# A two-direction graph-attention kernel: batch 0's self feature by block products, narrow matmuls for the key rows, and another order of a batch's loads

## The chip, the cores and the metric

The kernel runs on one core of a Trainium2 chip. A core has five engines that run their own instruction streams: TensorE (PE; its weight loads are listed apart as PEld), VectorE (DVE), ScalarE (ACT), GpSimd (POOL) and SyncE (SP), which here issues nearly all DMA transfers. Each engine works through its stream in order and waits on semaphores for the others. The metric is the device time of one execution in microseconds (us); less is better.

## The reference

For each of B = 16 batches there are N = 512 tokens of F = 512 features. A linear layer makes `self_feat` from the tokens and one condition vector per batch (left out for a token whose row sums to zero). Then come two graph attentions, one on the adjacency and one on its transpose. Each has H = 16 heads of width dh = 32, and only the first NG = 20 tokens are keys:

```python
row_zero = exp_v.sum(-1) == 0
q_exp = jnp.where(row_zero[..., None], 0.0, q[:, None, :])
self_feat = jnp.concatenate([exp_v, q_exp], -1) @ W_self.T + b_self
output = self_feat
for d in range(2):
    A = adj_f if d == 0 else jnp.swapaxes(adj_f, 1, 2)
    A = A[:, :, :NONGT, :]                       # B, N, 20 keys, 11 labels
    cond, vb = A.sum(-1), A @ w_bias + b_bias
    kv = self_feat[:, :20]
    qh = (self_feat @ Wq[d].T + bq[d]).reshape(B, N, H, dh)
    kh = (kv @ Wk[d].T + bk[d]).reshape(B, 20, H, dh)
    aff = jnp.einsum('bnhd,bmhd->bnhm', qh, kh) / sqrt(dh)
    aff = jnp.where(cond[:, :, None, :] > 0, aff, NEG) + vb[:, :, None, :]
    w = softmax(aff)
    out_t = jnp.einsum('bnhm,bmf->bnhf', w, kv)
    output += jnp.einsum('bnhf,hgf->bnhg', out_t, Wout[d]) + bout[d].reshape(H, -1)
return exp_v + relu(output)
```

All is fp32. The host passes x also transposed, and the adjacency already cut to the 2 x 20 columns that are used.

## The kernel before, in words

Features lie on the 128 partitions in C = 4 chunks, tokens in the free dimension. Instead of the queries, the kernel computes for each batch and head a key matrix folded with Wq (`g`, 608 columns in each of 4 chunks: 16 heads x 2 directions x 19 keys, the first key being subtracted from the others), so that the scores are one matmul of self_feat with `g`. Likewise the values are folded with Wout (`vd`). Work is written for each engine in program order under a manual schedule: the order in the code is the order on the engine.

*The setup* (L453 to 759) loads the weights, computes the key sums (`kv_terms`, L531 to 535: 16 matmuls of 128 x 320 into four banks, 320 = 16 batches x 20 keys) and the key rows (`key_rows(d, jc)`, L577 to 592: four matmuls of 128 x 320 into a bank, then ACT and DVE make `kh0` and `khD` from it). Then come 22 *bursts* (`keys(runs)`, L660 to 695), numbered n = 0 to 21. A burst is twelve short matmuls into two double banks. ACT copies one pair out (L684), DVE the other (L686) into `st`, which goes to the scratch `g_d` by DMA. From n = 4 on, fillers stand between the bursts, by the letters of the string `plan` (L714): b biases, c bias scores, n row flags (one matmul that gives `nz`), v and w values, s one step of the direct product for batch 0's self_feat (`self_feat`, L191 to 208: the F x 472 remaining token columns in four blocks of outputs x tokens; three blocks as fillers, the fourth, `self_feat(0, 1, 1)`, in the loop). `self_copy` (L210 to 218) adds the condition part on DVE when it takes a block from its bank. In the setup, banks come from a pool of four in turn (`bank(name)`); in the loop they are fixed (`bank(name, at)`).

*The loop* (L781 to 963) runs over batches b and four token tiles nt. For tile nt: `scores` (L353, 128 narrow matmuls), then on DVE `weigh` (add the mask term `full`, maximum, difference), exp on ACT, `normal` (sum, reciprocal, and the product on POOL), `turn` (transpose, L415). POOL's `full_add` makes `full` ahead of it. `attend` (L426) and `finish` (adds on DVE, relu on ACT) for batch b - 1 stand in nt 2 of batch b, the `residual` adds (POOL) and stores behind them. In the same tiles the next batch is prepared: the mask terms (`mask_mul` on ACT, `mask_count` and `mask_sum` on DVE), `new_self` (a small ACT copy) and self_feat by seven block products (`product(b, n)`, L246 to 279, of 2 x 2 blocks, in the order n = 1, 2, 6, 7, 5, 4, 3). The operands are sums of blocks that POOL makes (`x_sum` for the tokens, `weight_sums`, once, for the weights). Products 1, 6, 7 and 4 accumulate in two banks `ps_a`, product 2 in `ps_d`, 5 and 3 in `ps_c`. Between them DVE reads `ps_a` with `partial` (two instructions, L286; it adds the condition part and writes a tile `u`), and `joined` (one instruction, L296) adds `ps_d` or `ps_c` to `u` and writes the block of self_feat.

*The loads* of batch b + 1 go through SP's one queue, in program order, some held back until an instruction is done (`behind`): two of x (nt 0), the store of the row flags, `adj` first half (behind the masks), `nz` (nt 1, behind exp), four of `cq`, `adj` second half (behind `normal`), two of `xn` for batch b + 2 (nt 2, behind the first add and the first relu of `finish`), `g` first half (behind exp), two stores, `g` second half (nt 3, behind the masks), a store, four of `vd`, a store.

Of the kernel before, what the change touches and what calls it, by code (L numbers as in the profile page):

```python
# [18 lines left out]
def gat_kernel(  # L19
# [71 lines left out]
    adds, fulls, wts, outs, held, sf_ps, conds, prods = {}, {}, {}, [], [None] * 3, {}, {}, {}  # L91
    sums, parts, us, done = {}, {}, {}, {}
# [98 lines left out]
    def self_feat(b, f, h, parts=((0, range(C)), (1, range(C)))):  # L191


        lo, hi = max(NG, h * N // 2), (h + 1) * N // 2
        for i, ks in parts:
            if (i, ks[0]) == (0, 0):
                if (f, h) == (0, 0):
                    new_self(b)
                held[0] = bank(f"ps_sf{b}_{f}{h}", 3 if (f, h) == (1, 1) else None)
            for k in ks:  # L200
                for a in range(HL):
                    nc.tensor.matmul(  # L202
                        held[0][bass.ts(a, R), i * N // 2 : i * N // 2 + hi - lo],
                        ws_v[:, k, bass.ds((2 * f + i) * P + a * R, R)], xs[b][:, k, lo:hi],
                        start=(k == 0), stop=(k == C - 1),
                    )
            if (i, ks[-1]) == (1, C - 1):
                sf_ps[b, f, h] = held[0]

    def self_copy(b, f, h):  # L210

        lo, hi = max(NG, h * N // 2), (h + 1) * N // 2
        ps = sf_ps.pop((b, f, h))
        for i in range(2):
            nc.vector.scalar_tensor_tensor(
                sfs[b][:, 2 * f + i, lo:hi], nzs[b][:, lo:hi], qw[:, 2 * f + i, b : b + 1],
                ps[:, i * N // 2 : i * N // 2 + hi - lo], ALU.mult, ALU.add,
            )

# [15 lines left out]
    def x_sum(b, n):  # L235

        t = sums[b, n] = xsum.tile([P, 2, HN], F32, tag=f"t{n}", name=f"t{b}_{n}")
        one, two = {
            1: lambda: (x_block(b, 0, 1), x_block(b, 0, 0)),
            2: lambda: (x_block(b, 1, 1), sums[b, 1]),  # L240
            3: lambda: (x_block(b, 1, 1), x_block(b, 0, 1)),
            4: lambda: (x_block(b, 1, 0), sums[b, 2]),
        }[n]()
        nc.gpsimd.tensor_sub(t, one, two)  # L244

    def product(b, n):  # L246
# [11 lines left out]
        if n == 1:  # L258
            parts[b, "a"] = [bank(f"ps_a{b}_{i}", i) for i in range(2)]
        if n == 2:  # L260
            parts[b, "d"] = bank(f"ps_d{b}", 2)
        if n == 5:
            parts[b, "c"] = bank(f"ps_c{b}", 3)
# [17 lines left out]
    def partial(b, n, f, l, to=None):  # L281

        if to is None:
            to = us[b, n] = xsum.tile([P, 2, HN], F32, tag=f"u{n}", name=f"u{b}_{n}")
# [9 lines left out]
    def joined(b, n, key, f, l):  # L294

        nc.vector.tensor_add(  # L296
            block(b, f, l), parts[b, key][:, : 2 * HN].rearrange("p (i n) -> p i n", i=2), us.pop((b, n))
# [155 lines left out]
    with tc.tile_pool(name="setup", bufs=1) as sp, tc.tile_pool(name="ps_acc", bufs=4, space=PSUM) as acc["pool"]:  # L453
# [18 lines left out]
        with tc.tile_pool(name="setup_k", bufs=1) as sk:  # L472
# [58 lines left out]
            def kv_terms(fc, k):  # L531
                nc.tensor.matmul(  # L532
                    kv_ps[fc][:, :BM], ws_v[:, k, bass.ts(fc, P)], xkv[:, k],
                    start=(k == 0), stop=(k == C - 1),
                )
# [41 lines left out]
            def key_rows(d, jc):  # L577

                ps = bank(f"ps_k{d}{jc}")
                for k in range(C):  # L580
                    nc.tensor.matmul(  # L581
                        ps[:, :BM], wk_sb[d][:, k, bass.ts(jc, P)], kvT[:, k],
                        start=(k == 0), stop=(k == C - 1),
                    )
# [26 lines left out]
        with tc.tile_pool(name="setup_g", bufs=4) as sg:  # L611
# [85 lines left out]
            def self_step(b, f, h, i, k):  # L697
                self_feat(b, f, h, ((i, (k,)),))
                if (i, k) == (1, C - 1):
                    self_copy(b, f, h)  # L700
# [6 lines left out]
                "s": [  # L707
                    (self_step, (0, f, h, i, k)) for f, h in ((0, 0), (1, 0), (0, 1))
                    for i in range(2) for k in range(C)
                ],  # L710
# [3 lines left out]
            plan = "bvv vv vv ccw vv ns ssss sssw vv vv ssss ssss vv vv nww ssss ssss".split()  # L714
# [13 lines left out]
            for n, runs in enumerate(bursts):  # L728
# [40 lines left out]
    with tc.manual_schedule():  # L769
# [11 lines left out]
        for b in range(B):  # L781
# [7 lines left out]
            for nt in range(NT):  # L789
# [22 lines left out]
                if nt == 0:  # L812
# [4 lines left out]
                    else:  # L817
# [5 lines left out]
                        partial(b, 4, 1, 0, block(b, 1, 0))  # L823
# [8 lines left out]
                        joined(b, 3, "c", 1, 1)  # L832
# [21 lines left out]
                if nt == 1:  # L854
                    if b > 0:
                        joined(b, 2, "c", 0, 1)
# [189 lines left out]
```

## Time and profile before

| | us |
|---|---|
| median of 3 runs | 591.52 (590.48 to 591.87) |
| the profiled execution's own time | 593.27 |
| its span, first to last instruction | 591.5 |
| TensorE busy | 578.7 (98% of the span) |
| VectorE busy | 492.3 (83%) |
| ScalarE busy | 395.6 (67%) |
| GpSimd busy | 384.2 (65%) |
| setup, bursts with fillers (41.1 to 92.5) | 51.4 |
| loop from batch 0's last tile on (129.4 to 560) | 430.6 |

The times come from one profiled execution. Its chain is the work that ended last, followed back at each step to what released it. A row of the chain gives start, duration, engine, tile and line; "issue" is time in which an engine waited for nothing that the profile shows. A row of the timeline gives start, duration, engine, line, operation, output <- inputs, shape, count and, in brackets, the idle time before it with what ended it. A row of windows gives the stretch, its length, then busy time (and number) of PE, PEld, DVE, ACT and POOL, the granted clock of TensorE, the DMA engines' mean share and GB/s. A DMA row gives the count, KB each and the median us from issue to landing.

### The profile page before, as it was taken

To read this page: it belongs to the slowest core of one execution; us is meant where nothing else is said; L and a number is where in the kernel's file an instruction comes from. 1 tells how busy PE (TensorE), PEld (TensorE's weight loads), DVE (VectorE), ACT (ScalarE), POOL (GpSimd) and SP (SyncE) were. 2 spreads that over 40 slices of the span, in tenths; PEclk is the share of its full clock that TensorE was granted. 3 is DMA by queue.
4 is the path that set the end of the run, shared out by engine and by line. 5 is a ranking of instruction groups with operands and counts; after the bars stand their busy time and mean duration, and the time that the engine had idled before them with its cause. 6 is when DMAs were issued, how large, how long until landed. Compare 5 with 4: busy or idle time off the path is not lost.

```text
span 591.5 us, 30038 instructions
## 1 busy us (share of the span) xinstructions
PE 578.7 (98%) x13180; PEld 439.7 (74%) x13180; DVE 492.3 (83%) x785; ACT 395.6 (67%) x1162; POOL 384.2 (65%) x351
## 2 busy tenths in 40 slices
PE   8999999999999999999999999999999999999994
PEld 6654547888978687787878787788787878787882
DVE  0495565889898888999999999888989898989896
ACT  1234644587877677768686868677787877777661
POOL 2315663638677675758686777675858677776774
PEclk9999999999999999999999999999999999999997
DMA  8998999857848485767676766757585748582503
GB/s 294 385 406 299 332 376 329 257 126 199 223 154 229 155 236 148 206 168 209 184 208 163 223 173 202 171 181 208 164 217 170 216 149 232 158 238 85 167 13 142
DMA packets 98129, 124.10 MB, mean 210 GB/s; under 512 B 19952, under 2 KB 70160, under 8 KB 95952
## 3 DMA queue, kind: packets, MB, share of 16 engines
q1 hardware_dynamic: 96752, 120.31, 67.1%
q8 instruction: 103, 1.69, 1.2%
q0 software_dynamic: 672, 1.36, 1.0%
q10 hardware_dynamic: 576, 0.53, 0.3%
q14 instruction: 26, 0.21, 0.1%
HBM read 82.30 MB, written 40.24 MB: 207 GB/s over the span
## 4 chain that ended last, share of the span: by engine, by line
PE 94%; DVE 3%; DMA 1%; issue 1%; ACT 0%; POOL 0%; SPq 0%; DVEq 0%; POOLq 0%; ACTq 0%
PE ps_s L353 44%; PE ps_a L279 17%; PE ps_c L279 8%; PE ps_o L426 6%; PE ps_d L279 4%; PE ps_v L644 3%; PE ps_k L581 3%; PE ps_sf L202 2%; DMA ws_q<-in_wsT 1%; PE ps_kv L532 1%; DVE o L435 0%; PE ps_nz L186 0%; DVE wt L415 0%; DVE ps_s L371 0%; DVE sm L406 0%
## 5 line engine op out<-in xcount | busy, mean ns | idle before, releaser
L353 PEld LDWEIGHTS ps_s<-g,sf 128*32 128x32 f32 x8192 | 264.0, 110 | 19.8 <-issue 12.2
L353 PE MATMUL ps_s<-g,sf 128*32 128x152 f32 x8192 | 277.3, 293 | 0.5 <-ACT st L684 0.5
L334 ACT COPY both<-add 32x80 f32<-32x80 f32 x512 | 130.9, 256 | 54.8 <-DVE add L325 49.0
L408 POOL TENSOR_TENSOR s<-s,sm 128x640 f32<-128x640 f32 x63 | 80.3, 1275 | 98.0 <-DVE sm L407 98.0
L341 POOL TENSOR_TENSOR full<-cq,both 128x640 f32<-128x640 f32 x64 | 100.1, 1565 | 30.3 <-issue 24.3
L314 ACT ACTIVATE prod<-adj,wb_sb 128x80 f32<-128x80 int32 x330 | 112.5, 432 | 0.0
L380 ACT ACTIVATE s<-s 128x640 f32<-128x640 f32 x63 | 46.5, 738 | 69.4 <-DVE s L375 69.0
L444 POOL TENSOR_TENSOR o<-o,x 128x512 f32<-128x512 f32 x60 | 75.9, 1285 | 0.0
L367 DVE TENSOR_TENSOR full<-ps_s,full 128x608 f32<-128x608 f32 x63 | 49.1, 779 | 32.1 <-PE ps_s L353 26.6
L406 DVE TENSOR_REDUCE sm<-s 128x32 f32<-128x640 f32 x63 | 50.9, 808 | 8.8 <-ACT s L380 8.6
L279 PE MATMUL ps_a<-t,ws_s 128*32 128x246 f32 x960 | 55.5, 370 | 0.0
L371 DVE TENSOR_REDUCE ps_s<-full 128x32 f32<-128x640 f32 x63 | 52.2, 828 | 2.2
L415 DVE STREAM_TRANSPOSE wt<-s 128x640 f32<-128x640 f32 x63 | 52.8, 839 | 0.1
L375 DVE TENSOR_TENSOR s<-full,ps_s 128x640 f32<-128x640 f32 x63 | 51.6, 818 | 1.1
L426 PE MATMUL ps_o<-wt,vd 32*32 32x512 f32 (+5 forms) x816 | 40.8, 581 | 3.7 <-DVE wt L400 2.0
L279 PEld LDWEIGHTS ps_a<-t,ws_s 128*32 128x32 f32 x960 | 32.2, 110 | 15.5
L325 DVE TENSOR_REDUCE add<-prod 128x80 f32<-128x960 f32 x32 | 36.8, 1150 | 6.3 <-ACT prod L314 4.4
L244 POOL TENSOR_TENSOR t<-x 128x492 f32<-128x492 f32 x30 | 34.4, 1148 | 10.1 <-DVE full L367 5.2
L439 ACT ACTIVATE o<-o,bo 128x512 f32<-128x512 f32 x60 | 38.2, 708 | 0.6 <-POOL biased L881 0.6
L435 DVE TENSOR_TENSOR o<-ps_o,sf 128x512 f32<-128x512 f32 x60 | 36.8, 672 | 1.0 <-PE ps_o L426 1.0
L286 DVE SCALAR_TENSOR_TENSOR u<-nz,qw,ps_a 128x246 f32<-128x246 f32 x90 | 36.6, 449 | 0.0
L244 POOL TENSOR_TENSOR t<-x,t 128x492 f32<-128x492 f32 x30 | 34.4, 1147 | 1.2
(238 smaller groups left out, 722.7 us busy)
## 6 DMA issues: line engine op xcount, KB each, us to landing
g_d<-st SPq DMA_DIRECT2D x16, 1064.0 KB, 5.9
g<-g_d SPq DMA_DIRECT2D x28, 608.0 KB, 5.2
out_T<-o SPq DMA_DIRECT2D x60, 256.0 KB, 4.7
xn<-in_xn SPq DMA_DIRECT2D x28, 512.0 KB, 3.6
x<-in_xT SPq DMA_DIRECT2D x28, 512.0 KB, 4.3
adj<-in_adj SPq DMA_DIRECT2D x32, 440.0 KB, 5.0
nz<-nz_d SPq DMA_DIRECT2D x14, 256.0 KB, 4.0
wk<-in_wkT SPq DMA_DIRECT2D x2, 1024.0 KB, 8.0
```

The lines of the kernel that those rows point to most:

```text
L244: nc.gpsimd.tensor_sub(t, one, two)
L279: nc.tensor.matmul(to, lhs, x[:, k], start=start, stop=stop, skip_group_check=n != 2)
L314: nc.scalar.activation(p[:, :, l], a[:, :, l], AF.Identity, scale=wb_sb[:, l : l + 1])
L334: nc.scalar.copy(adds[b, h][bass.ts(a, R), :, g], add[r].rearrange("p (t m) -> p t m", t=2))
L341: nc.gpsimd.tensor_add(f, cqs[b].unsqueeze(1).to_broadcast(shape), adds[b, nt // 2][:, nt % 2].unsqueeze(2).to_broadcast(shape),)
L353: nc.tensor.matmul(bank[bass.ts(a, R), bass.ts(j, WD // HL)], sfs[b][:, k, bass.ds(nt * P + (2 * g + j) * R, R)], keys[:, k, a], start=(k ...
L371: nc.vector.tensor_reduce(mx, f, AX.X, ALU.max)
L375: nc.vector.tensor_sub(s, f, mx.unsqueeze(3).to_broadcast(full))
L408: done["normal"] = nc.gpsimd.tensor_mul(s, s, sm.unsqueeze(3).to_broadcast(full))
L415: nc.vector.transpose(wts[b][:, nt], s.rearrange("p a h m -> p (a h m)"))
L426: nc.tensor.matmul(banks[a][bass.ds(at // 2 * DH, n * DH)].rearrange("p (t n) -> p t n", n=32), vd[r, bass.ds(at * DH, n * DH)], wt[r, :, ...
L444: nc.gpsimd.tensor_add(o[:, c], o[:, c], xs[b][:, c])
```

## The change

Four things change.

- Key sums and key rows: each 128-output matmul becomes four of 32 outputs with the same 320 columns (16 become 64, 32 become 128).
- Batch 0's self_feat: the direct product and its two functions go. In the setup, seven `product(0, n)` stand behind bursts 14 to 20 (letter p), with `partial` and `joined` in between; the values are drawn together ahead of them. `weight_sums` and `row_sums(1)` move to n = 9, batch 0's `x_sum` calls and `new_self(0)` stand at n = 11; batch 0's sums lie in a tile `t0` of the pool of self_feat tiles.
- `partial` writes into the block of self_feat itself and `joined` adds to it in place; the tiles `u` are gone. `new_self(b + 1)` moves from nt 3 to nt 2, ahead of exp on ACT.
- Loads: `adj` first half without a wait right behind x (nt 0); `nz` in nt 2, behind exp(b, 1); `xn` behind the last add of `finish`; `store()` after the first two residuals; then `adj` second half and `cq`, both without a wait of their own; then `g` second half.

```diff
-    def self_feat(b, f, h, parts=((0, range(C)), (1, range(C)))):
...
-    def self_copy(b, f, h):
...
     def x_sum(b, n):
-        t = sums[b, n] = xsum.tile([P, 2, HN], F32, tag=f"t{n}", name=f"t{b}_{n}")
+        if b > 0:
+            t = xsum.tile([P, 2, HN], F32, tag=f"t{n}", name=f"t{b}_{n}")
+        else:
+            if n == 1:
+                held[0] = sfp.tile([P, C, N], F32, tag="sf", name="t0")
+            t = held[0][:, n - 1, : 2 * HN].rearrange("p (k n) -> p k n", k=2)
+        sums[b, n] = t
...
-    def partial(b, n, f, l, to=None):
-        if to is None:
-            to = us[b, n] = xsum.tile([P, 2, HN], F32, tag=f"u{n}", name=f"u{b}_{n}")
+    def partial(b, f, l):
+        to = block(b, f, l)
...
-    def joined(b, n, key, f, l):
+    def joined(b, key, f, l):
         nc.vector.tensor_add(
-            block(b, f, l), parts[b, key][:, : 2 * HN].rearrange("p (i n) -> p i n", i=2), us.pop((b, n))
+            block(b, f, l), parts[b, key][:, : 2 * HN].rearrange("p (i n) -> p i n", i=2), block(b, f, l)
         )
...
             add = nc.vector.tensor_add(o[:, c], banks[c], sfs[b][:, c])
-            if c == 0:
-                done["add"] = add
+            done["add"] = add
...
             def kv_terms(fc, k):
-                nc.tensor.matmul(
-                    kv_ps[fc][:, :BM], ws_v[:, k, bass.ts(fc, P)], xkv[:, k],
-                    start=(k == 0), stop=(k == C - 1),
-                )
+                for a in range(HL):
+                    nc.tensor.matmul(
+                        kv_ps[fc][bass.ts(a, R), :BM], ws_v[:, k, bass.ds(fc * P + a * R, R)], xkv[:, k],
+                        start=(k == 0), stop=(k == C - 1),
+                    )
...
                 for k in range(C):
-                    nc.tensor.matmul(
-                        ps[:, :BM], wk_sb[d][:, k, bass.ts(jc, P)], kvT[:, k],
-                        start=(k == 0), stop=(k == C - 1),
-                    )
+                    for a in range(HL):
+                        nc.tensor.matmul(
+                            ps[bass.ts(a, R), :BM], wk_sb[d][:, k, bass.ds(jc * P + a * R, R)], kvT[:, k],
+                            start=(k == 0), stop=(k == C - 1),
+                        )
...
+            def block_product(n):
+                first = {
+                    2: (partial, (0, 0, 0)), 6: (joined, (0, "d", 0, 0)), 7: (partial, (0, 0, 1)),
+                    4: (partial, (0, 1, 1)), 3: (joined, (0, "c", 1, 1)),
+                }
+                if n in first:
+                    f, args = first[n]
+                    f(*args)
+                product(0, n)
+                if n == 3:
+                    partial(0, 1, 0)
+                    joined(0, "c", 0, 1)
...
-            plan = "bvv vv vv ccw vv ns ssss sssw vv vv ssss ssss vv vv nww ssss ssss".split()
+            plan = "bvv vvc vvc vvn vv vvw vv vv ww wn p p p p p p p".split()
...
+                if n == 9:
+                    row_sums(1)
+                    weight_sums()
                 if n == 11:
-                    row_sums(1)
-                if n == 13:
-                    weight_sums()
+                    new_self(0)
+                    for i in range(1, 5):
+                        x_sum(0, i)
...
                             load_x(b + 1, range(2, C), done["partial"])
+                            load_adj(b + 1, 0)
...
-                        if more:
-                            load_adj(b + 1, 0, done["masks"])
...
-                    if b > 0 and more:
-                        load_nz(b + 1, done["exp"])
-                        load_cq(b + 1)
                     normal(*prev)
-                    if b > 0 and more:
-                        load_adj(b + 1, 1, done["normal"])
-                    if b == 0:
-                        self_feat(0, 1, 1)
                     for g in range(2):
                         scores(b, nt, g, ps[g])
-                    if b == 0:
-                        self_copy(0, 1, 1)
...
                         finish(b - 1, o, banks)
+                        if more:
+                            load_nz(b + 1, done["exp"])
...
                         product(b + 1, 2)
-                    s = weigh(b, nt, pair, (lambda: partial(b + 1, 1, 0, 0)) if more else None)
+                        new_self(b + 1)
+                    s = weigh(b, nt, pair, (lambda: partial(b + 1, 0, 0)) if more else None)
...
                             residual(b - 1, c, o)
+                        store()
+                        if more:
+                            load_adj(b + 1, 1)
+                            load_cq(b + 1)
...
                     product(b + 1, 6)
-                    new_self(b + 1)
```

More of the change, by code (lines that the diff above doesn't have):

```diff
@@ L90, in gat_kernel @@
     xs, xns, rss, adjs, nzs, sfs, cqs, gs, vds = {}, {}, {}, {}, {}, {}, {}, {}, {}
-    adds, fulls, wts, outs, held, sf_ps, conds, prods = {}, {}, {}, [], [None] * 3, {}, {}, {}
-    sums, parts, us, done = {}, {}, {}, {}
+    adds, fulls, wts, outs, held, conds, prods = {}, {}, {}, [], [None] * 3, {}, {}
+    sums, parts, done = {}, {}, {}
     def behind(one, other):
@@ L258, in product @@
         if n == 1:
-            parts[b, "a"] = [bank(f"ps_a{b}_{i}", i) for i in range(2)]
+            parts[b, "a"] = [bank(f"ps_a{b}_{i}", i if b else None) for i in range(2)]
         if n == 2:
-            parts[b, "d"] = bank(f"ps_d{b}", 2)
+            parts[b, "d"] = bank(f"ps_d{b}", 2 if b else None)
         if n == 5:
-            parts[b, "c"] = bank(f"ps_c{b}", 3)
+            parts[b, "c"] = bank(f"ps_c{b}", 3 if b else None)
         for i in range(2):
@@ L706, in gat_kernel @@
                 "n": [(row_flags, (b,)) for b in range(2)],
[L707 to L710, printed above, removed]
+                "p": [(block_product, (n,)) for n in (1, 2, 6, 7, 5, 4, 3)],
                 "v": [(values, (t, (d,), k)) for t in range(2) for d in range(2) for k in range(C)],
@@ L822, in gat_kernel @@
                         normal(*prev)
-                        partial(b, 4, 1, 0, block(b, 1, 0))
+                        partial(b, 1, 0)
                         if more:
@@ L915, in gat_kernel @@
                     product(b + 1, 6)
-                    new_self(b + 1)
-                    joined(b + 1, 1, "d", 0, 0)
+                    joined(b + 1, "d", 0, 0)
                     x_sum(b + 1, 4)
@@ L922, in gat_kernel @@
                     normal(*prev)
-                    partial(b + 1, 2, 0, 1)
+                    partial(b + 1, 0, 1)
                     mask_sum(b + 1, 0)
@@ L931, in gat_kernel @@
                     product(b + 1, 5)
-                    s = weigh(b, nt, pair, lambda: partial(b + 1, 3, 1, 1))
+                    s = weigh(b, nt, pair, lambda: partial(b + 1, 1, 1))
                     expo(s)
```

30 lines of the change are left out of this document (2 added, 28 removed).

## The prediction, made before the result was known

> **What bounds the kernel now.** I read the page's busy shares and chain first, then the stages, then the chain row by row round each edit.
>
> ```profile
> span 591.5 us, 30038 instructions
> ...
> PE 578.7 (98%) x13180; PEld 439.7 (74%) x13180; DVE 492.3 (83%) x785; ACT 395.6 (67%) x1162; POOL 384.2 (65%) x351
> ...
> PE 94%; DVE 3%; DMA 1%; issue 1%; ACT 0%; POOL 0%; SPq 0%; DVEq 0%; POOLq 0%; ACTq 0%
> ```
>
> TensorE is busy 98% of the span and carries 94% of the chain. But a mean hides stages, so here are the second part of the setup (the bursts with fillers between them) and the loop:
>
> ```profile
> core 0: us, PE busy (x) PEld busy (x) DVE busy (x) ACT busy (x) POOL busy (x), PEclk, DMA share, GB/s
> 41.10:92.50 51.40, 50.85 (x532) 24.56 (x532) 31.05 (x58) 24.21 (x56) 29.71 (x34) 1.00 0.93 340
> 129.40:560.00 430.60, 429.20 (x10940) 340.66 (x10934) 388.78 (x601) 325.23 (x980) 306.89 (x265) 1.00 0.67 189
> ```
>
> TensorE has 0.55 us free in 51.4 us of setup and 1.4 us in 430.6 us of loop. So what is taken from its work counts in full, every new wait of it counts in full, and work of other engines or transfers counts only where TensorE comes to wait for it. The diff does not touch the tail behind 560; I leave it out.
>
> The sum is made against the profiled execution, 593.27 us (span 591.5), which is 1.75 us above the median of the three runs, 591.52. I work out a difference and add it to the median.
>
> **Part 1: batch 0's self_feat.** The chain from 57.40 to 100.31 (42.91 us), grouped, and three of the direct product's pieces and one block product of the loop:
>
> ```profile
> by line: PE ps_sf L202 33.2%; PE ps_v L644 24.5%; PE ps_s L353 10.1%; PE ps_nz L186 3.5%; PE ps_g(3, 3, 0, 0, 2)0_875 L669 2.2%; PE ps_g(2, 2, 1, 0, 2)0_688 L669 2.2%; PE ps_g(2, 0, 0, 1, 2)0_594 L669 2.2%; PE ps_g(3, 1, 1, 0, 2)0_809 L669
> ...
> 74.41 1.73 PE ps_sf L202 x32
> 89.67 1.86 PE ps_sf L202 x32
> 96.86 3.45 PE ps_sf L202 x64
> 108.58 1.66 PE ps_a L279 x32
> ```
>
> Removed: 33.2% of 42.91 = 14.2 us. Added: seven products, 1.66 us each where one follows work of its own kind. After a burst a group costs more: 3.45/2 = 1.73 undisturbed against 1.86 behind a burst for the same 256 columns, 0.13. So 7 x (1.66 + 0.13) = 12.5 us, and part 1 brings **-1.7 us** (bounds 7 x 1.86 = 13.0, so -1.2; 7 x 1.66 = 11.6, so -2.6). The three removed pieces of self_copy on DVE (L215) and the added partials and joins change DVE by little; where they stand is part 3. On POOL the row sums, weight sums and batch 0's four x sums now stand at bursts 9 and 11, ahead of the products at 14 to 20; POOL has 21.7 of the 51.4 us free, so I cost them at nothing. If that cover failed, product 6 (burst 16) would wait for its x sum.
>
> **Part 2: key sums and key rows with 32 outputs.** Four times the instructions, each a quarter as wide, for the same columns.
>
> ```profile
> 11.45 2.39 PE ps_kv L532 x8
> ...
> 15.18 2.25 PE ps_kv L532 x8
> ...
> 27.34 2.35 PE ps_k L581 x8
> ...
> 20.25 0.53 DVE L588 SCALAR_TENSOR_TENSOR khD<-ps_k,bk_sb,kh 128x304 f32<-128x304 f32 x1 [1.80 <-ACT kh L587]
> 22.40 0.53 DVE L588 SCALAR_TENSOR_TENSOR khD<-ps_k,bk_sb,kh 128x304 f32<-128x304 f32 x1 [1.62 <-ACT kh L587]
> ```
>
> Key rows follow each other every 22.40 - 20.25 = 2.15 us: 8 records of 320 columns, 269 ns a record. The block product of 32 outputs needs 1.66/8 = 207.5 ns for four narrow matmuls of 246 columns; by columns that is 270 ns for 320. So no streaming gain. What may change is the start behind a burst (2.35 against 2.15; four key rows stand so) and behind another shape (2.39 against 2.25; one group). Between a gain of all these starts (4 x 0.2 + 0.14 = -0.9) and a loss of as much as a narrow group pays behind a burst (0.13, four times, +0.5) I take **-0.2 us**, the middle.
>
> [...]
>
> **Part 3: new waits of TensorE in the setup.** In the loop other TensorE work lies between a block product and the next use of its bank. In the setup only one burst lies there. Products 7 (burst 17) and 4 (burst 19) write ps_a, which DVE must first have read by the two instructions of `partial`; product 3 (burst 20) writes ps_c, which `joined` must first have read. On DVE each of these stands behind that burst's copy to `st` (L686).
>
> ```profile
> 80.00 0.01 PE ps_g(3, 0, 1, 1, 2)1_787 L669 x2
> ...
> 80.11 1.17 DVE L686 TENSOR_SCALAR st<-ps_g(3, 0, 1, 1, 2)1_787 128x304 f32<-128x304 f32 x2 [0.69 <-PE ps_g(3, 0, 1, 1, 2)1_787 L669]
> ...
> L286 DVE SCALAR_TENSOR_TENSOR u<-nz,qw,ps_a x90: 371/464/470, 110.5 to 553.4; 128x246 f32<-128x246 f32 x90
> ...
> L296 DVE TENSOR_TENSOR sf<-ps_c,u x30: 629/646/664, 125.5 to 563.9; 128x492 f32<-128x492 f32 x30
> ```
>
> From the burst's end: 0.1 until the copies start, 1.17 for them, 0.46 for the first partial (the second bank is read while TensorE fills the first): 1.7 us idle, twice. For the join 0.1 + 1.17 + 0.65 = 1.9. Sum **+5.3 us**. Lower bound: the wait cannot fall below the copies, 3 x 1.2 = 3.6; upper: both partials and 0.1 for the release, 3 x 2.2 = 6.6. Product 6 (burst 16) also follows a partial, but product 2 (1.66) and a whole burst lie between, against 0.1 + 1.17 + 0.84 = 2.1: I take no wait, at worst 0.4. The next burst is not held up: its buffers come free before the partial does. The last partial and join run beside burst 21, for whose copies scores(0,0) waited before too, so I cost them at nothing; without that cover the partial would be 0.8 us on the path.
>
> **Part 4: batch 0 without the direct product in the loop.** The fourth block (3.45 us, L202 at 96.86) gave POOL and DVE time between scores(0,0) and scores(0,1).
>
> ```profile
> 105.31 1.56 POOL L341 TENSOR_TENSOR full<-cq,both 128x640 f32<-128x640 f32 x1
> ...
> 92.52 4.34 PE ps_s L353 x128
> ...
> 112.88 1.66 PE ps_a L279 x32
> ...
> 171.12 0.79 DVE L367 TENSOR_TENSOR full<-ps_s,full 128x608 f32<-128x608 f32 x1
> 171.95 0.83 DVE L371 TENSOR_REDUCE ps_s<-full 128x32 f32<-128x640 f32 x1
> 172.69 0.84 DVE L286 SCALAR_TENSOR_TENSOR u<-nz,qw,ps_a 128x246 f32<-128x246 f32 x2
> ```
>
> On POOL, full_add(0,2) ends at 106.87, 14.35 us after the scores start, and nothing before it depends on the fourth block. Behind it DVE has weigh's add and maximum (0.79 + 0.83, rows of batch 1) and the first partial (0.46): 16.5 with the hand-over. Product 6 of batch 1 writes the bank that this partial reads; it started at 112.88, so without the block it would start 112.88 - 92.52 - 3.45 = 16.9 after the scores, or 16.1 if a gap of 0.77 us in product 2 (110.66, below) goes too. So it waits 0 to 0.4, and scores(1,0) may wait 0.1 to 0.3 for a partial later. I take **+0.5 us** (bounds 0, and 1.5 if POOL runs an operation of 1.56 late).
>
> **Part 5: the loads.** In each of 14 batches nz's load moves from behind exp(b,0) to behind exp(b,1), cq and the second half of adj move from ahead of xn to between the two halves of g, the first half of adj loses its wait for the masks, and xn waits for the last add of `finish` instead of the first. On SP's queue in batch 1, with the exp:
>
> ```profile
> 161.85 0.34 SPq L175 DMA_DIRECT2D nz<-nz_d  x1
> 162.24 2.28 SPq L119 DMA_DIRECT2D cq<-cq_d  x4
> 164.86 0.39 SPq L114 DMA_DIRECT2D adj<-in_adj  x1
> ...
> 175.12 0.38 SPq L130 DMA_DIRECT2D g<-g_d  x1
> ...
> 179.42 0.38 SPq L130 DMA_DIRECT2D g<-g_d  x1
> ...
> 166.84 0.74 ACT L380 ACTIVATE s<-s 128x640 f32<-128x640 f32 x1 [2.87 <-DVE s L375]
> ...
> g<-g_d SPq DMA_DIRECT2D x28, 608.0 KB, 5.2
> ...
> nz<-nz_d SPq DMA_DIRECT2D x14, 256.0 KB, 4.0
> ...
> 185.09 4.13 PE ps_s L353 x128
> ```
>
> The second half of g is used when scores(2,0) turns to key chunks 2 and 3, at 185.09 + 2.07 = 187.2; it lands at 179.42 + 5.2 = 184.6. Slack 2.6 us. After, one adj (128 partitions x 2 x 440 int32, 450 KB) and four cq stand ahead of it. Their issues (0.39 + 2.28 = 2.7 us) fit between the stores behind 175.12 and 179.42; the adj is 1.3 us of transfer at the setup's 340 GB/s, and cq takes at most the 2.28 us of its issues. So the landing moves by 1.3 to 3.6 us against a slack of 2.6; small as cq is, I take the lower end. nz now issues after the exp, at 167.6, and lands 4.0 later, 171.6, ahead of its first reader, the partial at 172.69. xn is read by row_sum in nt 3, whose result TensorE does not need in this batch. I take **0**; the cover is 2.6 us for g and 1.1 for nz.
>
> Sum: -1.7 - 0.2 + 5.3 + 0.5 + 0 = **+3.9 us**: 591.52 + 3.9 = 595.4 (a profiled execution near 597.2). The likeliest's own range, with the bounds of parts 1 to 4 not all at one end: 593 to 598.5.
>
> **Rivals.**
>
> Late keys, slower still: with g's second half 3.6 - 2.6 = 1.0 us late in 14 batches, +14, so 609. For: the queue is one, and these transfers now stand in a row; against: cq is small. [...]
>
> The other side: some batches hold gaps of TensorE that no wait explains.
>
> ```profile
> 184.91:216.75 31.84, 31.45 (x789) 24.28 (x785) 28.14 (x44) 23.50 (x72) 22.00 (x20) 1.00 0.63 183
> ...
> 248.86:279.34 30.48, 30.48 (x789) 24.15 (x785) 27.72 (x44) 23.35 (x72) 21.86 (x20) 1.00 0.68 191
> ...
> sum 371.29, PE 369.89 PEld 291.33 DVE 335.03 ACT 279.61 POOL 263.94; mean PE 30.82 PEld 24.28 DVE 27.92 ACT 23.30 POOL 22.00
> ...
> 110.66 0.77 issue
> ...
> 196.06 0.39 issue
> ```
>
> A quiet batch takes 30.48, the first of these 31.84; over the twelve whole batches of the sum the excess is 371.29 - 12 x 30.48 = 5.5 us. The gap of 0.39 lies inside attend's matmuls, of which no engine and no transfer is the releaser. If the other arrangement of transfers and instructions removes all of them: 595.4 - 5.5 = 589.9. It decides once it brings 3.9 + 1.2 = 5.1. For: they come in some batches only; against: nothing in the diff aims at attend.
>
> The stalls hide: if DVE has read the banks before TensorE gets there, the sum is -1.7 - 0.2 = -1.9, so 589.6. For it speaks that DVE is 40% idle in the setup; against, that the copies stand ahead of the partial in its one queue.
>
> [...]
>
> **How the numbers follow.** Forecast 0.60; late keys 0.11; gaps go 0.12; stalls hide 0.08; narrow rate 0.01; the rest, 0.08, mixes these. 0.2% (1.2 us) is about what a measurement of this kernel can tell from no change. Faster (under 590.3): most of the gaps and of the hidden stalls, the narrow rate, 0.17. Same (to 592.7): 0.11, from what is left of these two and the mixtures. Slower: 0.72. The range, 589.3 to 602, takes in the gaps, the hidden stalls and keys that are a little late; it leaves out the narrow rate and keys late in full.
>
> **What would show it.** Of part 3: three waits of TensorE for DVE, 1.7, 1.7 and 1.9 us, ahead of products 7, 4 and 3. Of part 2: key rows still 2.15 to 2.35 us apart. Of part 1: 1.7 to 1.8 us per product. Scores(0,0) would start some 6.8 us later than 92.52 (three blocks of 14.2 - 3.45 = 10.8 us become seven products of 12.5, and the waits come on top). Of part 5: batches of 30.5 us, with no wait for g or nz. Wrong would be: no such waits in the setup, or waits for transfers in the loop.

## The result

| | before | after |
|---|---|---|
| median | 591.30 us (6 runs, 590.36 to 592.32) | 605.97 us (6 runs, 603.71 to 612.52) |
| the profiled execution | 593.27 us, span 591.5 | 603.71 us, span 601.9 |

The changed kernel is slower: ratio 1.0263, 95% interval 1.0214 to 1.0312, some 14.7 us. The forecast was 595.4, in a range up to 602. The page of the changed kernel:

```profile
span 601.9 us, 30531 instructions
...
PE 576.2 (96%) x13436; PEld 432.8 (72%) x13436; DVE 493.0 (82%) x788; ACT 396.1 (66%) x1162; POOL 389.0 (65%) x355
```

TensorE has 2.5 us less to do (576.2 against 578.7 us) in a span that is 10.4 us longer, so it waits more. Its own list of waits (total us, times, longest), cut to the first six lines:

```profile
PE ps_s L329 <- issue: 7.0, 7, 2.1
PE ps_d L256 <- issue: 2.2, 1, 2.2
PE ps_o L402 <- DVE wt L376: 2.0, 1, 2.0
PE ps_c L256 <- DVE sf L272: 2.0, 1, 2.0
PE ps_a L256 <- POOL g L670: 1.8, 1, 1.8
PE ps_a L256 <- DVE sf L262: 1.8, 1, 1.8
```

Two kinds are new or grown. Three waits of 1.8, 1.8 and 2.0 us for a bank (the last line but one is named after an operation of POOL that ended near it; the bank is read by L262) are those of the setup. They stand ahead of products 7, 4 and 3 in the timeline:

```profile
83.28 1.87 PE L256 MATMUL ps_a<-t,ws_s 128*32 128x246 f32 x32 [1.79 <-DVE sf L262]
...
90.71 1.87 PE L256 MATMUL ps_a<-t,ws_v 128*32 128x246 f32 x32 [1.79 <-POOL g L670]
...
95.52 1.87 PE L256 MATMUL ps_c<-x,ws_s 128*32 128x246 f32 x32 [1.96 <-DVE sf L272]
```

The other kind, 9.2 us of "issue" in the lines shown and 0.6 in one further down, has no releaser. Before, TensorE's list held 1.4 + 0.8 us of it:

```profile
PE ps_o L426 <- issue: 1.4, 3, 0.5
PE ps_d L279 <- issue: 0.8, 1, 0.8
```

The span, cut at the first scores and at the start of product 2 of each next batch (both from the timeline of TensorE):

| us | before | after | difference |
|---|---|---|---|
| start to scores(0,0) | 92.52 | 98.37 | +5.85 |
| from there to product 2 of batch 1 | 17.54 | 15.02 | -2.52 |
| 14 periods, product 2 to product 2 | 433.69 | 439.69 | +6.00 |
| from there to the end | 47.75 | 48.82 | +1.07 |

So the setup went about as forecast, and the loop lost 6 us where I had taken nothing. One of its gaps in the chain, tile 1 of a batch:

```profile
352.00 1.55 PE ps_s L329 x48
353.55 2.06 issue
355.61 1.45 PE ps_s L329 x37
```

TensorE stops in the middle of 128 like matmuls, and the profile shows nothing that it waits for. What came late is seen in the list of DMA queues, cut to two stretches. First the 12 us ahead of it (340.8 to 352.8; columns: packets, MB, share of the 16 engines):

```profile
q1 hardware_dynamic: 2955, 3.37, 88.3%
q8 instruction: 1, 0.02, 0.5%
q14 instruction: 1, 0.01, 0.2%
```

And the 13 us from 353 on:

```profile
q1 hardware_dynamic: 244, 0.53, 11.9%
q8 instruction: 4, 0.07, 2.4%
```

Queue q8 carries instructions: 106 packets and 1.74 MB in the whole run, 16.4 KB each. If q8 is TensorE's program, its 13,436 matmuls and 13,436 weight loads take 64 to 65 bytes each by division (the kernel before: 26,360 of them and 1.69 MB), some 254 to a packet; the counts below give 256, which is 4.13 us of scores. Here one packet came in 12 us, then four in 13. Packets began at 340.7, 346.3, 353.3 and 356.7. The gap began 7 us behind the second of these and ended 2 us behind the third. The other long gaps of the loop (291.55, 479.85, 541.41) have the same picture: the packet ahead of the restart began 6.8, 7.1 and 5.9 us after the one before it.

That q8 is what TensorE stopped for can be counted in the trace. Take the four restarts, and count all instructions of TensorE's stream (matmuls, weight loads, semaphore instructions) that had started before them and the packets of q8 that had landed:

| restart, us | gap | packets landed | last of them landed | instructions started |
|---|---|---|---|---|
| 292.99 | 1.44 | 46 | 291.51 | 11,969 |
| 355.61 | 2.06 | 58 | 354.37 | 15,041 |
| 481.06 | 1.21 | 83 | 479.61 | 21,441 |
| 542.38 | 0.96 | 95 | 541.03 | 24,513 |

Each count is 256 times the packets, plus 193. So TensorE stopped where the landed packets ended, and went on 1.2 to 1.5 us after the next one. In the traces of all fourteen kernels of this document there are 67 "issue" gaps of matmuls; 65 stand at 256 times the packets plus 193 or 194, and end 1.2 to 1.6 us behind a landing. (The other two are a wait for a partial, see part 4 below.) The packets behind which there is a gap began when at most 127 of the instructions already landed were left, half of them with 62 or fewer; the 1,262 others between 95 and 570 us with 200 in the median and never more than 286. In these traces a packet of TensorE's program thus usually began with somewhat less than a packet (200 of 256 instructions) still to run. The two medians lie 138 instructions apart, which is 2.2 us of scores: by that estimate a packet that begins some 2 us later than usual stops TensorE. The two windows around the gap at 353.55 (last columns: granted clock, DMA share, GB/s) show how the new order packs the transfers:

```profile
338.00:353.00 15.00, 14.78 (x375) 12.77 (x369) 12.90 (x21) 11.19 (x39) 11.02 (x10) 1.00 0.91 287
353.00:363.00 10.00, 7.94 (x227) 5.84 (x219) 6.70 (x11) 4.64 (x14) 5.08 (x4) 1.00 0.03 8
```

Fifteen microseconds at 0.91 of the DMA engines, then ten at 0.03. My theory from here on, A: the loop's loss is TensorE's instruction fetches, late where transfers are packed; the setup's loss is the three waits.

### The profile page after: what moved, and what is told of

It reads as the page before. It is cut to its first block, busy times and chain, and to the rows that moved or that the text cites. A ratio compares the mean times of both kernels' runs of the same rounds, so it can differ in the third digit from the quotient of the medians.

```text
span 601.9 us, 30531 instructions
## 1 busy us (share of the span) xinstructions
PE 576.2 (96%) x13436; PEld 432.8 (72%) x13436; DVE 493.0 (82%) x788; ACT 396.1 (66%) x1162; POOL 389.0 (65%) x355
## 3 DMA queue, kind: packets, MB, share of 16 engines
q8 instruction: 106, 1.74, 1.2%
## 4 chain that ended last, share of the span: by engine, by line
PE 78%; DVE 3%; issue 2%; ACT 0%; POOL 0%; DVEq 0%; POOLq 0%; ACTq 0%
PE ps_s L329 43%; PE ps_a L256 17%; PE ps_c L256 9%; PE ps_o L402 5%; PE ps_d L256 4%; DVE o L411 0%; DVE wt L391 0%; DVE ps_s L347 0%; DVE sm L382 0%; DVE full L343 0%; POOL s L384 0%; DVE st L663 0%; DVE s L373 0%; DVE sm L371 0%; DVE s L351 0%
## 5 line engine op out<-in xcount | busy, mean ns | idle before, releaser
L329 PE MATMUL ps_s<-g,sf 128*32 128x152 f32 x8192 | 281.2, 293 | 7.7 <-issue 7.0
L256 PE MATMUL ps_a<-t,ws_s 128*32 128x246 f32 x1024 | 60.3, 371 | 2.4 <-DVE sf L262 1.8
L262 DVE SCALAR_TENSOR_TENSOR sf<-nz,qw,ps_a 128x246 f32<-128x246 f32 x128 | 51.4, 442 | 0.6 <-PE ps_a L256 0.6
L221 POOL TENSOR_TENSOR t<-x 128x492 f32<-128x492 f32 x32 | 36.8, 1150 | 20.5 <-DMA x<-in_xT 12.3
L256 PEld LDWEIGHTS ps_a<-t,ws_s 128*32 128x32 f32 x1024 | 34.6, 110 | 19.8 <-POOL g L670 2.2
L166 ACT ACTIVATE xn<-xn 128x512 f32<-128x512 f32 x56 | 34.5, 618 | 6.6 <-DMA xn<-in_xn 6.5
L402 PE MATMUL ps_o<-wt,vd 32*32 32x512 f32 (+5 forms) x816 | 36.7, 579 | 2.3 <-DVE wt L376 2.0
L221 POOL TENSOR_TENSOR t<-x,t 128x492 f32<-128x492 f32 x32 | 36.7, 1147 | 1.3
```

The source lines that it names most:

```text
L256: nc.tensor.matmul(to, lhs, x[:, k], start=start, stop=stop, skip_group_check=n != 2)
L329: nc.tensor.matmul(bank[bass.ts(a, R), bass.ts(j, WD // HL)], sfs[b][:, k, bass.ds(nt * P + (2 * g + j) * R, R)], keys[:, k, a], start=(k ...
L402: nc.tensor.matmul(banks[a][bass.ds(at // 2 * DH, n * DH)].rearrange("p (t n) -> p t n", n=32), vd[r, bass.ds(at * DH, n * DH)], wt[r, :, ...
```

## The experiments

**The loads, both ways.** First the changed kernel with the old order of loads (`e1_old_loads`; its edit in short, with the places in remarks):

```diff
-                            load_adj(b + 1, 0)                     # nt 0, behind x
+                            load_adj(b + 1, 0, done["masks"])      # nt 0, behind mask_sum
+                        load_nz(b + 1, done["exp"]); load_cq(b + 1)          # nt 1
+                        load_adj(b + 1, 1, done["normal"])                   # nt 1
-                            load_nz(b + 1, done["exp"])                      # nt 2
-                        store(); load_adj(b + 1, 1); load_cq(b + 1)          # nt 2
-            done["add"] = add                    # last add
+            if c == 0: done["add"] = add         # first add
```

> The changed kernel with the loads (and only the loads) in the order and with the waits of the kernel before. Theory A, fetches: TensorE's own instructions come by transfers of about 16 KB each (queue q8), every gap of TensorE in the changed kernel's loop stands 1 to 2 us behind one that came 6 to 9 us after the one ahead of it, and these late ones stand where the new order packs the DMA engines full. Then the loop goes back to the gaps of before, the three stalls of the setup (1.8, 1.8 and 2.0 us) stay, and the time is 594 to 598. Rival B: the loop is slower because of TensorE's changed program (more and other instructions), whatever the loads: 603 to 607. Rival C: data that lands late (keys, cq, x); then waits of TensorE for a transfer or for DVE go with the loads, and the time also falls to 594 to 598, but such waits would have to stand in the loop of the changed kernel, and its list of waits has none.

Then the kernel before with the new order, the same edit reversed (`e2_new_loads`):

> The kernel before with only the loads in the new order. Theory A (fetches late where transfers are packed): 598 to 603, with gaps of 0.5 to 2 us in several batches that no wait explains, each behind a fetch that came 6 us or more after the one ahead. Rival B (TensorE's program): 590 to 593.

Measured: 601.11 us for the first (ratio 1.0152, 1.0117 to 1.0187) and 596.51 for the second (1.0097, 1.0062 to 1.0131). The second is a little under the 598 to 603 that I expected. Rival B falls with it as the main cause: the new order alone costs some 5 us with TensorE's program as before. TensorE's waits there:

```profile
PE ps_s L353 <- issue: 6.9, 8, 2.1
...
PE ps_d L279 <- issue: 1.3, 1, 1.3
...
PE ps_s L353 <- DMA g<-g_d: 0.2, 1, 0.2
```

Its 14 periods take 440.27 us, 6.6 more than before. Of this 0.2 us is a wait for data (g), so late keys, my rival of the prediction, are nearly nothing.

The first missed its expectation by 3 us or more, though its loop did what A says: "issue" in TensorE's list is 1.0 us in scores, beside one gap of 2.4 us in product 2 of batch 1, and the 14 periods take 434.21 (433.69 before). (That early gap comes with the changed setup: between 90 and 122 us every profile with that setup has 1.8 to 3.2 us of fetch gaps, under either order of loads, those with the old setup 0.3 to 1.3.) The loss is ahead of the loop: scores(0,0) start at 102.89, 4.5 us later than in the changed kernel, with the same three waits. The windows of 3.4 us from 82 on show why; the third column from the right is the granted clock:

```profile
82.00:85.40 3.40, 1.61 (x32) 0.94 (x29) 2.63 (x5) 1.01 (x2) 0.87 (x2) 1.00 1.00 399
85.40:88.80 3.40, 3.40 (x67) 1.98 (x56) 1.17 (x2) 1.01 (x2) 0.53 (x2) 1.00 0.95 376
88.80:92.20 3.40, 1.61 (x29) 0.86 (x25) 1.93 (x4) 1.01 (x2) 1.61 (x2) 0.99 0.90 361
92.20:95.60 3.40, 3.40 (x35) 1.75 (x31) 0.00 (x0) 0.00 (x0) 0.00 (x0) 0.51 0.88 351
95.60:99.00 3.40, 1.43 (x28) 0.93 (x32) 2.33 (x5) 1.00 (x2) 1.03 (x2) 1.00 0.10 31
99.00:102.40 3.40, 3.37 (x36) 1.44 (x28) 0.85 (x2) 0.00 (x0) 0.79 (x1) 0.50 0.01 1
```

Behind the second and the third wait TensorE's granted clock is halved for 3.4 us, and in those stretches it does 35 and 36 matmuls instead of 67. Each costs some 1.7 us: from product 1 (74.20) to scores(0,0) it takes 28.69 us, in the changed kernel (73.08 to 98.37) 25.29. The other 1.1 of the 4.5 us lie ahead of product 1. The whole run's mean clock is 0.989 to 0.990 in all four executions of this kernel. Of the six of the changed kernel three have 0.993 to 0.996 (603.71, 605.56 and 605.27 us; the profiled one is among them, so no trace of this kernel shows the halving) and three 0.988 to 0.990 (606.38, 612.52 and 607.53). The kernel before has 0.993 to 0.997 throughout. TensorE was busy 1.61 of the 3.4 us ahead of the first halved stretch and 1.43 ahead of the second. In the window from 82.0 it was also busy 1.61, and the clock behind it stayed at 1.00; I can't say from these runs what sets the difference.

**Is it the idling that halves the clock?** `e6_fill` keeps the old loads and the three waits, and puts spare work into them:

```diff
+                if n in (7, 4, 3):
+                    spare_product()   # 32 narrow matmuls like product 2, into ps_d, which nobody reads any more
                 product(0, n)
```

> The run with the old loads, with 32 spare narrow matmuls (a copy of product 2, into a bank nobody reads any more) put into each of the three stalls of the setup. The wait for the bank stays as long, but TensorE is busy in it for about 1.8 of the 1.8 to 2.0 us. If idling is what lowers the granted clock: no 0.50 in the setup, a granted clock of 0.995 over the run, scores(0,0) near 98.5 instead of 102.9, and 596 to 598. If the clock falls for another reason (place in the program, the transfers): 601 to 603, clock 0.989.

Measured: 596.64 us (ratio 1.0067, 1.0042 to 1.0092). The windows of the same part:

```profile
85.00:88.40 3.40, 3.40 (x64) 1.95 (x60) 1.18 (x2) 1.02 (x2) 1.62 (x2) 1.00 0.87 345
88.40:91.80 3.40, 3.40 (x64) 2.06 (x64) 1.93 (x4) 1.01 (x2) 0.52 (x2) 1.00 0.92 363
91.80:95.20 3.40, 3.24 (x60) 1.71 (x55) 1.85 (x4) 1.00 (x2) 0.55 (x2) 1.00 0.65 263
```

96 matmuls of no use, nothing else changed against the run with the old loads, and the kernel is 4.5 us faster in the median: the clock stays at 1.00, scores(0,0) start at 98.01, 25.30 us behind product 1. By the two traces 3.4 us of the 4.5 are the clock. So in the run with the old loads the idle time costs twice, once as such (the three waits, 5.5 us in the changed kernel) and once through the clock behind it (3.4 us).

**Taking the waits away.** `e4_drain` is the changed kernel, new loads included, with DVE's read of a product's bank ahead of the next burst's copies:

```diff
-                first = {2: (partial, ...), 6: (joined, ...), 7: ..., 4: ..., 3: ...}   # behind keys(runs)
+            drains = {15: (partial, (0, 0, 0)), 16: (joined, (0, "d", 0, 0)), 17: (partial, (0, 0, 1)),
+                      19: (partial, (0, 1, 1)), 20: (joined, (0, "c", 1, 1))}
...
+                if n in drains:
+                    drains[n][0](*drains[n][1])
                 keys(runs)
```

> The changed kernel, with the partial or join that reads a product's bank put ahead of the next burst's copies on DVE instead of behind them. By the three waits in its setup (1.79, 1.79 and 1.96 us): 5.0 to 5.6 us less than the changed kernel, 600 to 601, and no wait of TensorE for DVE ahead of products 7, 4 and 3. Rival: the copies then come late and the bursts wait for them, no gain: 604 to 607.

Measured: 595.51 us (ratio 1.0061, 1.0041 to 1.0081), 10.5 less than the changed kernel and more than the 5 to 5.6 that I expected. In four of the five executions the clock stays up as well (0.994 to 0.997). The fifth has 0.988 and took 605.22 us; it has no trace, so where its clock fell isn't known; it fell without the three waits. In the profile scores(0,0) start at 92.00. TensorE's waits:

```profile
PE ps_s L329 <- issue: 5.7, 6, 1.9
...
PE ps_a L256 <- DVE sf L262: 0.8, 1, 0.8
PE ps_s L329 <- DMA g<-g_d: 0.7, 2, 0.3
```

The three waits of the setup are gone, the gaps of the loop stay (14 periods: 439.75 us). The new order's cost is thus there whether or not the setup idles. Two waits that the prediction priced show up small: waits of product 6 for a partial (0.8 us here in batch 1; that of part 4 stands in batch 0, see there), and one for g of 0.7 us in all.

**Transfers that nobody waits for.** If gaps come from packed DMA engines, useless transfers must cause them too. `e3_spare` adds two such copies per batch to the kernel before:

```diff
+    def copy_spare(b, h):
+        nc.sync.dma_start(spare[h], a)        # one half of adj, HBM to HBM
...
                             load_x(b + 1, range(2, C), done["partial"])
+                            copy_spare(b + 1, 0)
...
                             residual(b - 1, c, o)
+                        if more:
+                            copy_spare(b + 1, 1)
```

> The kernel before, all its loads in place, with two copies of 450 KB each from HBM to HBM added per batch, which nobody reads, at the two places where the changed kernel has the halves of adj (behind x, and behind the first two residuals). Theory A: 596 to 610, by gaps of TensorE behind late fetches, without a wait of TensorE for data. Rival C (late data): no slower than 593 unless a wait for g or cq shows on TensorE's list. Rival B: 590 to 593.

`e9_no_out` goes the other way: the new order in the kernel before, with the stores of the output of batches 0 to 13 left out, so its time is that of a kernel with less to move.

```diff
         for b, c, o in outs:
-            nc.sync.dma_start(out[b, bass.ts(c, P)], o[:, c])
+            if b >= B - 2:
+                nc.sync.dma_start(out[b, bass.ts(c, P)], o[:, c])
```

> The kernel before with all loads in the new order (the run that took 596.51), and without the stores of the output of batches 0 to 13: 1 MB less per batch, three of the four stores of a batch standing among the transfers that the new order packs. All loads, waits and TensorE's program stay. Theory A (a fetch is late because the transfers around it fill the DMA engines): the gaps go, 588 to 592. If the order itself does it (a load behind another on the one queue, a wait that moves): 595 to 598, unchanged.

Measured: 598.64 us with the spare copies (ratio 1.0101, 1.0069 to 1.0134) and 588.51 without the stores (0.9964, 0.9946 to 0.9982). With the copies, TensorE's waits hold no transfer, but:

```profile
PE ps_s L358 <- issue: 3.1, 3, 1.3
PE ps_c L284 <- issue: 2.3, 3, 1.8
```

and its 14 periods take 439.92 us. Without the stores they take 430.64, under the kernel before. The same stretch of the two runs with the new order, with all stores and then without, and of the kernel before (columns as above, busy PE first):

```profile
99.00:530.00 431.00, 422.54 (x10757) 337.81 (x10753) 380.71 (x589) 321.21 (x972) 297.60 (x258) 1.00 0.61 190
```

```profile
99.00:530.00 431.00, 429.82 (x11012) 348.32 (x11008) 388.42 (x600) 328.07 (x992) 303.69 (x264) 1.00 0.53 163
```

```profile
99.00:530.00 431.00, 428.83 (x10930) 342.73 (x10923) 386.30 (x596) 324.86 (x982) 302.34 (x264) 1.00 0.69 194
```

TensorE is idle 8.5 us of this stretch with the stores, 1.2 without. The order of the loads, their waits and TensorE's program are equal, so the gaps hang on the transfers around the fetches and not on any single load. But the mean share of the DMA engines (the last column but one) doesn't set them: of the three it is highest in the kernel before (0.69), which idles 2.2 us. What goes with the gaps is how long the engines are full at a stretch. Of all stretches of 4 us between 130 and 550 us (one every 0.5 us), those with a DMA share over 0.9, beside the mean share and TensorE's "issue" gaps in the same time:

| | mean share | stretches over 0.9 | gaps, us |
|---|---|---|---|
| before | 0.67 | 16% | 1.4 |
| after | 0.60 | 27% | 6.3 |
| e1: after, old loads | 0.65 | 14% | 0.2 |
| e2: before, new loads | 0.59 | 24% | 6.9 |
| e3: before, spare copies | 0.70 | 33% | 5.8 |
| e9: before, new loads, stores left out | 0.51 | 5% | 0.5 |

That the late thing is the instruction packet itself is shown by the counts above; no run moves the packets alone. The copies and the stores are issued on the queue that carries the loads, so whether full engines or that queue's backlog holds a packet back isn't told apart.

**Which loads.** `e7_adj0_early` moves only the first half of adj (behind x, no wait for the masks), `e8_rest_late` everything but that:

```diff
+                            load_adj(b + 1, 0)                     # e7 only
-                            load_adj(b + 1, 0, done["masks"])      # e7 only
```

> The kernel before with one load moved: the first half of adj for the next batch goes out right behind x, without the wait for the masks. If late fetches come from this transfer being packed behind x, vd and the stores: 594 to 597, most of the loss of all new loads (596.5). If they come from the loads between the halves of g: 590 to 592.5.

> The kernel before with the other loads moved (nz behind exp of nt 1, second half of adj and cq between the halves of g, xn behind the last add) and the first half of adj left in its place. The complement of the run before: 590 to 592.5 if the first half of adj is what matters, 594 to 597 if the loads between the halves of g are; about 593.5 in both if it is the sum that counts.

Measured: 590.79 us (ratio 0.9990, 0.9968 to 1.0012) and 595.11 (1.0054, 1.0030 to 1.0079). The first half of adj costs nothing by itself (its 14 periods, 429.36 us, are the shortest of all profiles here); the loads put between the halves of g, with nz and xn, cost 3.5 of the 5 us. The table's measures go the same way: 13% of the stretches over 0.9 and 0.7 us of gaps in the first, 27% and 2.8 us in the second.

**What is left, and the width of the key rows.** `e5_drain_old` is the changed kernel with both corrections. Three more, with wide key rows and key sums (`e10_wide`), with those and adj early (`e11_wide_adj0`), and narrow with adj early (`e12_narrow_adj0`), use the edits shown and the matmuls of the kernel before.

> The changed kernel with both corrections: loads as before, and the partials and joins ahead of the next burst's copies. What is left of the change is the seven products, the narrow key rows and the work in place. The run with the old loads (601.11) had a quiet loop, but the granted clock fell to 0.50 behind two of its three stalls. Theory A (stalls, halved clock behind them, late fetches: each cause gone with its correction): scores(0,0) start near 92.0 as in the run with the drained banks, the loop as in the run with the old loads, so 588.5 to 590.5, a little under the kernel before. Rival B (TensorE's changed program slows the loop by itself): 593 or more.

> The changed kernel with both corrections (591.64) and the key sums and key rows again as matmuls of 128 outputs, a quarter of the instructions. By the rows of the changed kernel a narrow key row takes 2.15 us as a wide one does, so by streaming alone no difference: 591 to 592. By theory A the narrow form has TensorE fetch some 288 instructions (one block of 16 KB) more in the setup, and the gap in product 2 of batch 1 (0.77 us before, 1.85 with the narrow form) shrinks: about 1 us less, 590 to 591.

> The run beside it with wide key rows, and the first half of adj for the next batch right behind x (in the kernel before that move gave 590.79, and its profile a loop with fewer gaps). If the two add: 589 to 590.5, the fastest of all. If that move changes nothing: the same as the run beside it.

> The changed kernel with both corrections (591.64) and the first half of adj right behind x, key rows narrow. With the three runs beside it this makes a square: what the width of the key rows and what the place of adj are worth, each measured twice. Theory A: 0.5 to 1.5 us slower than the same with wide key rows, 590 to 591.5.

| | median, us | ratio to before | 95% interval |
|---|---|---|---|
| e5: narrow | 591.64 | 0.9981 | 0.9958 to 1.0004 |
| e10: wide | 590.23 | 0.9997 | 0.9980 to 1.0014 |
| e11: wide, adj early | 592.80 | 1.0040 | 1.0019 to 1.0061 |
| e12: narrow, adj early | 589.31 | 0.9993 | 0.9967 to 1.0019 |

(The ratio goes by runs of the same chip.) With both corrections the change is worth nothing that can be measured; I had expected 588.5 to 590.5 for e5. E11 (589 to 590.5 expected) came out slower and e12 (590 to 591.5) faster than I thought. In the profiles scores(0,0) start at 91.61 (e5) to 93.06 (e10) against 92.52, though seven products replace three blocks of the four; the way from there to product 2 of batch 1 is 14.65 against 17.54; and the 14 periods take 433.51. That profiled execution has a span of 588.0, but the eleven runs go from 587.70 to 592.35. My expectation for wide rows (1 us less) shows neither way: wide is faster without the early adj and slower with it, so the width is worth less than the gaps vary (the fetch gaps are 5.0 us in the profile of e11 and 1.9 in that of e12). (The narrow form has 288 matmuls and as many weight loads more, 106 packets against 103, not the one block that I had reckoned.) None of these beats both kernels beyond its interval.

## Why the prediction was wrong

Step by step:

- *Part 1* (products, 1.66 + 0.13): right. In the changed kernel product 1 takes from 73.08 to the next burst at 74.87, 1.79 us.
- *Part 2* (no gain from narrow matmuls): right. DVE takes the key rows at 20.16 and 22.31, 2.15 apart as before; behind a burst the group takes 2.36 us against 2.42. The "narrow rate" of the chances (0.01), narrow matmuls at four times the rate, is shown by no run: four matmuls of 32 outputs took the place of one of 128, and take as long (the first four key rows 9.02 us against 9.10).
- *Part 3* (three waits, 5.3 us): right in place and size, 1.79 + 1.79 + 1.96 = 5.54. What the step lacked is the clock: with the old loads the halved stretches behind the waits cost 4.5 us more (601.11 against 596.64 with the waits filled; 3.4 by the traces), and half of the executions of the changed kernel have the lower mean clock too.
- *Part 4* (0.5 us for a partial in batch 0): right in place and size where it shows. In the run with drained banks product 6 of batch 1 waits 0.51 us (at 108.74, while the partial that starts at 108.17 reads the bank), in e12 0.43; the list calls both "issue", and they are the two gaps that stand at no packet's end. In the changed kernel a fetch gap of 2.17 us in product 2 of batch 1 covers it.
- *Part 5* (loads, taken at **0**, "the cover is 2.6 us for g and 1.1 for nz") is the step that failed. As far as it goes it holds: waits for g are 0 to 0.7 us in all runs with the new order, and TensorE's list has none for nz. But I asked only which data the new order would bring late. A user of the same DMA engines with no line in the kernel, TensorE's own program, wasn't on my list: with the loads alone it costs 5.2 us (596.51).
- The rival "gaps go" named the right place (gaps that no wait explains) and the wrong sign. I had seen the gaps and the DMA queue named "instruction" in the page of before, and didn't lay the times of the one beside the other.

The sum by experiments: new loads +5.2; the waits without the clock, less what the products save, +5.0 (the filled run); the clock up to +4.5 (3.4 by the traces). That makes 10.2 without the clock and 14.7 with it, against 14.7 in the median. But executions of the changed kernel with a high clock already took 603.7 to 605.6 us, 2 to 4 more than the 601.5 that the first two make; the profile has 2.9 us of fetch gaps behind scores(0,0) (before 0.8, the filled run 2.0). The rest is open.

## What to carry to other kernels

Here an engine's program was a transfer like any other. TensorE, the bound, took 4.13 us of scores for the 256 instructions of one packet of 16.4 KB, and the new order of the loads alone, with late packets and only 0.2 us of waiting for data, cost 5.2 us. In such a kernel look at the "instruction" queue beside the gaps marked "issue", and keep the DMA load even over a batch rather than asking only whether each load lands in time; the mean share didn't show the difference (0.67 with 1.4 us of gaps before, 0.59 with 6.9 in e2). When work is put between bursts, let the engine that drains a bank read it ahead of its copies of the next burst: behind the copies it made TensorE wait 1.79, 1.79 and 1.96 us here; read ahead of them (e4), these three waits were gone. A short idle stretch of TensorE can cost as much again through the clock: in the trace of e1 two waits of 1.79 and 1.97 us cost some 1.7 us each that way, in that of the changed kernel the clock behind the same waits stayed at 1.00. Filling them with useless matmuls was worth 4.5 us.

## What was not expected of the hardware

- TensorE ran out of instructions where the DMA engines stayed full: 65 gaps of 0.2 to 2.4 us in fourteen traces stand exactly where the landed packets of 16.4 KB (256 instructions) ended, and 1.2 to 1.6 us passed from the next landing to the restart. Over the 6 us ahead of a packet that came too late the DMA share was 0.87 in the mean, ahead of the others 0.63. The order of the loads alone cost 5.2 us (596.51 against 591.30).
- Behind waits of 1.79 and 1.97 us in the trace of e1 the granted clock was 0.51 and 0.50 for 3.4 us. No other trace shows it; the mean clock that goes with it (0.988 to 0.990) came in all four executions of that kernel, in three of six of the changed one and in one of five of e4.
